# A fused two-layer graph kernel: the setup and first group rewritten, with a step table of its own

## The chip, the cores and the metric

The kernel runs on one core of one Trainium2 chip. Its time is the device time of one execution in microseconds (us). Before the change the median of three runs is 1575.77 us (1575.29 to 1577.64). The profile is of one further execution.

A core has five engines that run side by side, each through a queue of its own in order: TensorE (PE in the profile; PEld are its weight loads), VectorE (DVE), ScalarE (ACT), GpSimd (POOL) and SyncE (SP), which here only issues DMAs. An instruction at the head of a queue that waits for another engine holds everything behind it.

## What is computed

For each of 128 graphs of 128 nodes with 256 features:

```python
h = relu(layernorm(x))
x = x + adj @ (h @ W0) + b0                            # layer 0
h = relu(layernorm(x))
f = h @ fc_w + fc_b                                    # 8 heads of 256
logits = (f @ q_w + q_b) + (f @ k_w + k_b).T           # for each head
a = softmax(leaky_relu(logits + (1 - adj) * -1e9))
x = x + sigmoid(concat(a @ f) @ fp_w + fp_b + h)       # layer 1
```

All is float32. The kernel never makes f. The weights are folded first: for each head, q_w and k_w are multiplied into fc_w (the columns `wqk`), and fc_w times fp_w gives the 256x256 matrices held in `wts`.

## The kernel before

**Groups and periods.** Four graphs make a group (`GB`), so there are 32 groups, s0 to s31. A setup, written out by hand, loads and turns the weights and takes the first groups some way. Then a loop runs over the groups, one period each. A period has 44 slots, four units of 11; a unit is two graphs times half of the heads (`ORDER`, L595). In every slot PE does either one `aggregate` (L561: attention times h, output g_ps) or one `multiply` (L599: eight products with the folded weights of one of seven factors f0 to f6). The multiplies of a unit run in the slots of the next unit, so unit 0 of the first period has none. `take` (L572) turns g_ps into the factors: on ACT, or for (1, 0) on DVE with a difference on POOL. `combine` (L617) adds the sums up on DVE.

**The step table.** Beside the slots stands `PLAN` (L673): (slot, which group relative to the current one, step, arguments). In period g the attention of group g + 1 is made, the first layer of group g + 3 is computed, the second norm of g + 2 is applied, and so on. The loop (L906 to L935) first issues the slot's PE work, then the steps of that slot in the table's order. This order, by hand, is the order in every queue (the schedule is set to manual at L760). In the first period (g = 0) the steps in `LATE` (L756) are left out of PLAN, and `FIRST_PLAN` (L869) adds others for s0, s1, s2 and s3.

**Attention of one graph.** `masked` (L494) spreads the k values with a 32x32 block transpose on DVE (L489) and adds the mask, also on DVE (L497). `leaky` (L507) is eight ACT instructions, `head_max` (L515) one DVE reduction, `exps` (L523) eight ACT instructions, `normal` (L531) a small DVE reciprocal and a product on POOL (L535). `move` (L539) then carries the attention of two graphs, in 32x32 blocks, into another tile by 16 DMAs on SP (those of s0's first pair on SP and ACT), so that `turn` (L550), a DVE block transpose, makes a full transpose of it. h2 is turned the same way by `move_h2` and `turn_h2_blocks` (L421, L428), adj by `load_blocks` and `turn_blocks` (L73, L346). `turn_h2` (L435) and `turn_adj` (L352) do the same by PE transposes and ACT copies; before the change they are used for s0 and s1. `make_qk`, `turn_qk` and `load_k` (L448 to L481) make q and k, send k to memory on SP and read it back spread over the partitions (kq), which `masked` needs.

**The setup.** `setup_turn` (L171) transposes fc_w. `setup_wqk` (L183) makes wqk with 16 products for each half of the features, of two columns each. `setup_weights` (L207) folds fc_w and fp_w for one head and half and copies from PSUM on DVE or ACT. `setup_fb` (DVE, one block of fp_w at a time) and `setup_fb2` (POOL, the last blocks at once, L250) fold the bias; `NV` (L239) says where they part. `setup_sums` (L271) makes sums of the folded weights on POOL and DVE in turn.

PSUM tiles with the tag "m" share six banks (`ps_m`). Input tiles (xg, ag) have two buffers, so that the load of group n waits for the end of the first layer of group n - 2.

## Time and profile before

| | before |
|---|---|
| median of three runs | 1575.77 us |
| the profiled execution | 1576.38 us |
| its span, first to last instruction | 1574.2 us |
| mean granted TensorE clock | 0.979 |
| busy: PE, PEld | 1509.0, 1213.2 us |
| busy: DVE, ACT, POOL | 1228.9, 1173.8, 984.0 us |
| DMA moved | 142.07 MB, mean 90 GB/s |
| first masking of s0 (L489) starts | 42.56 us |
| first g_ps of the first period (L564) starts | 74.70 us |
| first take (L581) starts | 79.92 us |
| first masking of the second period (L489) starts | 146.83 us |

How to read it: "busy" is the time in which an engine executed, over the span. The page also cuts the span into 40 equal slices of some 39 us and prints the busy share of each in tenths, so a row of 9s is an engine that is busy throughout. "PEclk" is the TensorE clock that was granted, also in tenths. The stage table sums the same for stretches that one chooses, with the number of instructions in brackets. In the timeline a row is: start in us, duration or, for merged instructions, the stretch from first to last in us, engine, line of the kernel, operation, output<-inputs, shapes, count, and in square brackets how long the engine had been idle before and what ended that. SPq is SP's queue issuing DMAs. The chain of waits is the work that ended last, followed back from the end: each piece of it is what the next piece waited for.

### The profile page before, as it was taken

The numbers are of one execution on the slowest core, as the hardware profiler recorded it, in microseconds if no ns is written. First come the engines' busy times: TensorE is split into PE (matmuls) and PEld (weight loads), VectorE is DVE, ScalarE is ACT, GpSimd is POOL, SyncE is SP. The second block draws the span as 40 slices with busy tenths as digits, with TensorE's granted clock in tenths as the row PEclk, the third lists the DMA queues.
The fourth block names the chain that finished last, engine by engine and source line by source line (L and its number), as shares of the span: only waits on it lengthen the run. The fifth ranks groups of instructions, "written<-read, shape, count | busy, mean of one in ns | idle before, by whom it ended". The sixth has DMA issues, their size and how long they took to land.

```text
span 1574.2 us, 30745 instructions
## 1 busy us (share of the span) xinstructions
PE 1509.0 (96%) x9953; PEld 1213.2 (77%) x9953; DVE 1228.9 (78%) x2253; ACT 1173.8 (75%) x3889; POOL 984.0 (63%) x724
## 2 busy tenths in 40 slices
PE   7786999999999999999999999999999999999997
PEld 7565877887777878777777877777877777778776
DVE  5676778887777888777888877788887778887762
ACT  3683788777778877777987777897777789777751
POOL 3163766666676666676666667666666766666664
PEclk7888999999999999999999999999999999999999
DMA  5132434434444443444444344444434444433320
GB/s 181 34 88 63 104 84 97 94 90 88 101 93 97 95 93 78 102 104 90 97 93 95 80 102 105 87 98 92 94 82 101 107 83 98 92 78 80 73 68 27
DMA packets 259689, 142.07 MB, mean 90 GB/s; under 512 B 174901, under 2 KB 226505, under 8 KB 259273
## 3 DMA queue, kind: packets, MB, share of 16 engines
q1 hardware_dynamic: 259288, 139.79, 39.7%
q8 instruction: 78, 1.28, 0.4%
q14 instruction: 83, 0.67, 0.2%
q10 hardware_dynamic: 240, 0.33, 0.1%
HBM read 39.86 MB, written 17.30 MB: 36 GB/s over the span
## 4 chain that ended last, share of the span: by engine, by line
ACT 44%; PE 23%; DVE 16%; SPq 9%; issue 4%; DMA 2%; POOL 2%; ACTq 0%; POOLq 0%; DVEq 0%
ACT attn L526 18%; PE acc L609 11%; ACT attn L510 10%; SPq L546 6%; DVE attn L497 6%; ACT h L319 6%; PE x_ps L383 5%; PE g_ps L564 5%; DVE attn L489 5%; ACT f L589 2%; ACT L657 2%; ACT L526 2%; SPq L426 2%; ACT z L657 2%; DVE st L285 1%
## 5 line engine op out<-in xcount | busy, mean ns | idle before, releaser
L609 PEld LDWEIGHTS acc<-wts,f 128*128 128x128 f32 x7168 | 889.6, 192 | 281.2 <-issue 181.7
L609 PE MATMUL acc<-wts,f 128*128 128x128 f32 x7168 | 897.9, 276 | 23.8 <-DVE z L625 12.9
L564 PE MATMUL g_ps<-attnT,h 128*128 128x512 f32 x1024 | 530.1, 600 | 5.3 <-DVE attnT L553 3.3
L526 ACT ACTIVATE attn<-attn,nmax 128x128 f32<-128x128 f32 x1024 | 397.3, 396 | 0.4
L587 POOL TENSOR_TENSOR f<-f,f 128x512 f32<-128x512 f32 x128 | 163.2, 1275 | 286.7 <-DVE f L585 284.4
L510 ACT ACTIVATE attn<-attn,q 128x128 f32<-128x128 f32 x1024 | 312.9, 391 | 34.4 <-DVE attn L497 27.1
L535 POOL TENSOR_TENSOR attn<-attn,total 128x1024 f32<-128x1024 f32 x128 | 245.1, 1915 | 140.8 <-DVE total L534 140.8
L589 ACT COPY f<-g_ps 128x512 f32<-128x512 f32 x128 | 73.3, 572 | 241.1 <-PE g_ps L564 241.1
L518 DVE TENSOR_REDUCE nmax<-attn 128x8 f32<-128x1024 f32 x128 | 154.0, 1204 | 64.1 <-ACT attn L510 63.9
L526 ACT ACTIVATION_READ_ACCUMULATOR attn<-attn,nmax 128x1 f32 x1024 | 199.3, 195 | 0.0
L497 DVE TENSOR_TENSOR attn<-attn,mask 128x1024 f32<-128x1024 f32 x128 | 186.4, 1456 | 4.5
L590 POOL TENSOR_TENSOR f<-f,f 128x512 f32<-128x512 f32 x128 | 180.5, 1410 | 6.5 <-ACT f L589 3.9
L553 DVE STREAM_TRANSPOSE attnT<-attnB 128x1024 f32<-128x1024 f32 x128 | 153.3, 1218 | 39.7 <-DMA attnB<-attn 34.7
L489 DVE STREAM_TRANSPOSE attn<-kq 128x1024 f32<-128x1024 f32 x128 | 157.2, 1228 | 15.9 <-DMA kq<-k_mem 15.6
L564 PEld LDWEIGHTS g_ps<-attnT,h 128*128 128x128 f32 x1024 | 157.6, 194 | 13.8 <-issue 9.6
L383 PE MATMUL x_ps<-w_sb,ahT 128*128 128x256 f32 x512 | 124.2, 387 | 0.0
L585 DVE TENSOR_TENSOR f<-g_ps,f 128x512 f32<-128x512 f32 x128 | 87.1, 681 | 47.3 <-POOL attn L535 38.9
L661 POOL TENSOR_TENSOR z<-z,x 128x1024 f32<-128x1024 f32 (+1 forms) x33 | 76.2, 2310 | 56.3 <-ACT z L657 56.3
L653 POOL TENSOR_TENSOR z<-z,h 128x256 f32<-128x256 f32 x128 | 90.7, 731 | 23.3 <-DVE z L625 22.7
L581 ACT COPY f<-g_ps 128x512 f32<-128x512 f32 x128 | 74.0, 578 | 40.7 <-PE g_ps L564 39.6
L383 PEld LDWEIGHTS x_ps<-w_sb,ahT 128*128 128x128 f32 x512 | 93.5, 192 | 11.6 <-issue 0.7
L586 DVE TENSOR_TENSOR f<-f,g_ps 128x512 f32<-128x512 f32 x128 | 86.5, 676 | 0.0
(93 smaller groups left out, 1356.8 us busy)
## 6 DMA issues: line engine op xcount, KB each, us to landing
attnB<-attn SPq DMA_DIRECT2D x1019, 64.0 KB, 2.0
xg<-in_x_dram SPq DMA_DIRECT2D x32, 512.0 KB, 4.0
out_dram<-z SPq DMA_DIRECT2D x31, 512.0 KB, 3.1
h2B<-h SPq DMA_DIRECT2D x480, 32.0 KB, 1.9
ag<-in_adj_dram SPq DMA_DIRECT2D x32, 256.0 KB, 4.5
agB<-in_adj_dram SPq DMA_DIRECT2D x120, 64.0 KB, 4.5
fcw<-in_L_gnn_fc_w_dram SPq DMA_DIRECT2D x2, 1024.0 KB, 6.9
fpw<-in_L_gnn_fp_w_dram SPq DMA_DIRECT2D x1, 2048.0 KB, 14.1
```

The source lines that it names most:

```text
L383: nc.tensor.matmul(op[:, bb, :], lhsT=s["ahT"][:, 2 * b2 + bb, c, :], rhs=w0_sb[:, c, :], start=(c == 0), stop=(c == NC - 1),)
L489: nc.vector.transpose(s["a", b // 2][:, :, b % 2], s["kq"][:, :, b].unsqueeze(3).to_broadcast([P, NB, H, Q]),)
L497: nc.vector.tensor_tensor(a, a, s["mask"][:, b, :] .rearrange("p (j c) -> p j c", c=Q) .unsqueeze(2) .to_broadcast([P, NB, H, Q]), ALU.add,)
L510: nc.scalar.activation(a[:, :, h, :], a[:, :, h, :], AF.Prelu, bias=s["q"][:, b, h : h + 1], alpha=0.01,)
L518: nc.vector.tensor_reduce(nmax, a.rearrange("p j h c -> p h j c"), AX.XY, ALU.max, negate=True)
L526: nc.scalar.activation(a[:, :, h, :], a[:, :, h, :], AF.Exp, bias=s["nmax", b][:, h : h + 1], accum_out=s["total", b][:, h : h + 1],)
L535: nc.gpsimd.tensor_tensor(a, a, total.unsqueeze(1).unsqueeze(3).to_broadcast([P, NB, H, Q]), ALU.mult)
L553: nc.vector.transpose(aT.rearrange("p h (i r) -> p i h r", r=Q), s["ab", b // 2][:, :, b % 2])
L564: nc.tensor.matmul(u["g", b, c], lhsT=s["h2"][:, 2 * pair + b].rearrange("p j c q -> p (j c q)")[:, ts(c, P)], rhs=s["aT", 2 * pair + b][: ...
L587: nc.gpsimd.tensor_tensor(new(5), f[4], f[0], ALU.subtract)
L590: nc.gpsimd.tensor_tensor(new(2), f[1], f[5], ALU.subtract)
L609: nc.tensor.matmul(acc[:, slot, :], lhsT=u["f"][m][:, h, :], rhs=wt[m][:, half * HU + h, :], start=(half == 0 and h == 0 and m in FIRST), ...
```

## The change

The change rewrites the setup from `setup_wqk` on, gives the first period a complete table of its own, and leaves PLAN, which rules all later periods, as it is.

- `setup_wqk` makes rows instead of columns: for each half n of the heads and each g of four, 2 products with a 32-column stationary operand (`qkc`: q_w, k_w, and zeros) and 256 columns of fcwT, written to the partitions of column group g. `setup_wqk_turn` transposes the rows on PE into wqk_p.
- `NV` is NK - 8 instead of NK - 4: POOL's `setup_fb2` folds 8 blocks of the bias and DVE's `setup_fb` 8 instead of 12.
- s0's attention tile is laid out by heads (`view`), so that `turn_by_products` can transpose each head on PE, with one copy on ACT and one on DVE. s0 has no more `move` and `turn`. Other groups keep the layout by blocks.
- In the first period s2's adj and h2 are turned on PE (`turn_adj`, `turn_h2`), s3 takes the agB blocks, and s0's second half and all of s1's attention stand at new slots. In the setup the order of the folded weights, the bias, both `setup_sums` and s1's first layer is new.

The setup and the table before can be read in the listing above (L797 to L904).

```diff
--- before.py
+++ after.py
@@ -136,6 +136,9 @@
     cols = sp.tile([P, ROWS], FP, name="cols")
     mq = sp.tile([P, 1], FP, name="mq")
     mk = sp.tile([P, 1], FP, name="mk")
+    qkc = sp.tile([P, NC, Q], FP, name="qkc")
+    nc.gpsimd.memset(qkc, 0.0)
+    wqk_rows = sp.tile([P, 2, D], FP, name="wqk_rows")
     ones = sp.tile([P, P], FP, name="ones")
     nc.gpsimd.memset(ones, 1.0)
@@ -180,25 +183,38 @@
                 tp.rearrange("p k (j q) -> p k j q", q=Q),
             )
-    def setup_wqk(c):
-        qk_cols = cols[:, NK:ROWS].rearrange("p (two c) -> p c two", two=2)
-        wp = ps_m.tile([P, H, 2], FP, name="wp", tag="m")
-        for h in range(H):
-            for kk in range(NC):
-                nc.tensor.matmul(
-                    wp[:, h, :],
-                    lhsT=fcwT[:, NC * h + kk, ts(c, P)],
-                    rhs=qk_cols[:, kk, :],
-                    start=(kk == 0),
-                    stop=(kk == NC - 1),
-                )
+    def setup_wqk():
         nc.vector.tensor_copy(
-            wqk_p[:, c, 0 : 2 * H].rearrange("p (two h) -> p two h", two=2),
-            wp.rearrange("p h two -> p two h"),
-        )
-    def setup_wqk_order():
+            qkc[:, :, 0:2], cols[:, NK:ROWS].rearrange("p (two c) -> p c two", two=2)
+        )
+        wp = ps_m.tile([P, 2, D], FP, name="wp", tag="m")
+        for n in range(2):
+            for g in range(4):
+                for kk in range(NC):
+                    nc.tensor.matmul(
+                        wp[ts(g, Q), n, :],
+                        lhsT=qkc[:, kk, :],
+                        rhs=fcwT[:, NC * (4 * n + g) + kk, :],
+                        start=(kk == 0),
+                        stop=(kk == NC - 1),
+                    )
+        nc.vector.tensor_copy(wqk_rows, wp)
+    def setup_wqk_turn():
+        tp = ps_m.tile([P, 2, NC, P], FP, name="wt_ps", tag="m")
+        for n in range(2):
+            for c in range(NC):
+                nc.tensor.transpose(tp[:, n, c, :], wqk_rows[:, n, ts(c, P)], ident)
+        for c in range(NC):
+            nc.vector.tensor_copy(
+                wqk_p[:, c, 0 : 2 * H].rearrange("p (two n g) -> p n two g", two=2, n=2),
+                tp[:, :, c].rearrange("p n (g r) -> p n r g", r=Q)[:, :, 0:2],
+            )
+    def setup_wqk_order(_):
         for j in range(NB):
             for c in range(NC):
                 n = 2 * (j % 2) + c
@@ -236,7 +252,7 @@
-    NV = NK - 4
+    NV = NK - 8
     fb = sp.tile([P, D], FP, name="fb")
     fb2 = sp.tile([P, NK - NV, D], FP, name="fb2")
@@ -482,18 +498,27 @@
+    def view(s, b):
+        a = s["a", b // 2]
+        if s["g"]:
+            a = a.rearrange("p (j b h c) -> p b j h c", j=NB, b=2, c=Q)
+        else:
+            a = a.rearrange("p (b h j c) -> p b j h c", j=NB, b=2, c=Q)
+        s["v", b] = a[:, b % 2]
     def spread(s, b):
         if b % 2 == 0:
-            s["a", b // 2] = at.tile([P, NB, 2, H, Q], FP, name="attn", tag="attn", bufs=3)
+            s["a", b // 2] = at.tile([P, 2 * H * P], FP, name="attn", tag="attn", bufs=3)
+        view(s, b)
         nc.vector.transpose(
-            s["a", b // 2][:, :, b % 2],
+            s["v", b],
             s["kq"][:, :, b].unsqueeze(3).to_broadcast([P, NB, H, Q]),
         )
     def masked(s, b):
         spread(s, b)
-        a = s["a", b // 2][:, :, b % 2]
+        a = s["v", b]
         nc.vector.tensor_tensor(
             a,
             a,
...
@@ -544,7 +569,8 @@
         for n in blocks:
             i, j = divmod(n, NB)
             queues[n % len(queues)].dma_start(
-                s["ab", pair][ts(j, Q), i], s["a", pair][ts(i, Q), j]
+                s["ab", pair][ts(j, Q), i],
+                s["a", pair][ts(i, Q)].rearrange("p (j n) -> p j n", j=NB)[:, j],
             )
     def turn(s, b):
@@ -553,6 +579,17 @@
         nc.vector.transpose(
             aT.rearrange("p h (i r) -> p i h r", r=Q), s["ab", b // 2][:, :, b % 2]
         )
+    def turn_by_products(s, b):
+        aT = s["aT", b] = pool["attnT"].tile([P, H, P], FP, name="attnT", tag="attnT")
+        for h4 in range(2):
+            tp = ps_m.tile([P, 4, P], FP, name="aT_ps", tag="m")
+            for h in range(4):
+                n = H * (b % 2) + 4 * h4 + h
+                nc.tensor.transpose(tp[:, h, :], s["a", b // 2][:, ts(n, P)], ident)
+            copy = nc.vector.tensor_copy if h4 else nc.scalar.copy
+            copy(aT[:, ts(h4, 4)], tp)
@@ -753,7 +790,99 @@
         (43, 0, residual_a, 1),
     ]
-    LATE = (shift_both, n2_apply, move_h2, turn_h2_blocks, make_qk, turn_qk, load_k, turn)
+    FIRST_PLAN = [
+        (0, "u", take, 0, 0, 0),
+        (0, 3, load_blocks),
+        (0, 0, exps, 2, 0, H),
+        (3, "u", take, 0, 1, 1),
+        (3, 0, head_max, 3),
+        (7, "u", take, 0, 1, 0),
+        (9, "u", take, 0, 0, 1),
+        (9, 0, normal, 2),
+        (9, 0, exps, 3, 0, H),
+        (11, "u", take, 1, 0, 0),
+        (12, 2, turn_adj),
+        (12, 2, make_mask),
+        (14, "u", take, 1, 1, 1),
+        (14, 1, masked, 0),
+        (15, 0, normal, 3),
+        (15, 2, n1_apply, 0),
+        (15, 2, n1_apply, 1),
+        (15, 2, add_b0),
+        (16, 0, turn_by_products, 2),
+        (17, "u", take, 1, 1, 0),
+        (17, 1, leaky, 0),
+        (18, 0, turn_by_products, 3),
+        (18, 3, n1_stats, 0),
+        (18, 3, n1_stats, 1),
+        (20, "u", take, 1, 0, 1),
+        (20, 1, masked, 1),
+        (20, 2, first_a, 0),
+        (20, 2, first_a, 1),
+        (21, 0, residual_a, 0),
+        (22, "u", take, 2, 0, 0),
+        (22, 1, leaky, 1),
+        (22, 1, head_max, 0),
+        (22, 1, exps, 0, 0, H),
+        (23, 2, first_b, 0),
+        (23, 2, first_b, 1),
+        (24, 4, begin),
+        (24, 2, n2_stats, 0),
+        (24, 2, n2_stats, 1),
+        (24, 2, rdev_both),
+        (25, "u", take, 2, 1, 1),
+        (25, 1, head_max, 1),
+        (25, 1, normal, 0),
+        (25, 2, shift_both),
+        (26, 2, n2_apply, 0),
+        (26, 2, n2_apply, 1),
+        (26, 1, exps, 1, 0, H),
+        (26, 1, masked, 2),
+        (27, "u", combine, 1, 4),
+        (28, "u", take, 2, 1, 0),
+        (28, 2, turn_h2, 0),
+        (28, 2, turn_h2, 1),
+        (28, 1, normal, 1),
+        (28, 1, move, 0),
+        (28, 1, leaky, 2),
+        (31, "u", take, 2, 0, 1),
+        (31, 3, n1_apply, 0),
+        (31, 3, n1_apply, 1),
+        (31, 3, add_b0),
+        (31, 1, masked, 3),
+        (32, 2, make_qk, wqk_p),
+        (32, 1, head_max, 2),
+        (32, "u", combine, 1, 2),
+        (32, 0, residual_b, 0),
+        (33, "u", take, 3, 0, 0),
+        (33, 1, exps, 2, 0, H),
+        (33, 1, leaky, 3),
+        (34, 2, turn_qk),
+        (34, 2, load_k),
+        (34, 3, turn_blocks),
+        (36, "u", take, 3, 1, 1),
+        (36, 0, setup_wqk_order),
+        (36, 4, n1_stats, 0),
+        (36, 4, n1_stats, 1),
+        (36, 1, head_max, 3),
+        (36, 1, normal, 2),
+        (37, 3, first_a, 0),
+        (37, 3, first_a, 1),
+        (37, 1, exps, 3, 0, H),
+        (38, 1, turn, 0),
+        (39, "u", take, 3, 1, 0),
+        (39, 3, first_b, 0),
+        (39, 3, n2_stats, 0),
+        (39, 1, turn, 1),
+        (39, 1, normal, 3),
+        (40, 1, move, 1),
+        (41, 3, first_b, 1),
+        (41, 3, n2_stats, 1),
+        (41, 3, rdev_both),
+        (42, "u", take, 3, 0, 1),
+        (42, 3, make_mask),
+        (43, 0, residual_a, 1),
+    ]
     groups = [{"g": g} for g in range(NG)]
     pool = {}
@@ -794,114 +923,83 @@
     pool["attnT"] = ctx.enter_context(tc.tile_pool(name="attnT", bufs=4, side="right"))
     n2_apply(s0, 0)
     n2_apply(s0, 1)
+    setup_wqk()
     for half in range(2):
         n1_stats(s1, half)
     scale((s1, "n1"), root=True)
+    turn_h2(s0, 0)
+    turn_h2(s0, 1)
+    setup_wqk_turn()
     setup_bias()
     begin(s2)
-    setup_fb2()
-    for k in range(NV):
-        setup_fb(k)
-    setup_wqk(0)
-    turn_h2(s0, 0)
-    turn_h2(s0, 1)
-    setup_wqk(1)
+    for half in range(2):
+        n1_apply(s1, half)
+    make_mask(s1)
+    add_b0(s1)
     make_qk(s0, wqk_p)
+    turn_adj(s1)
     turn_qk(s0)
     load_k(s0)
-    for half in range(2):
-        n1_apply(s1, half)
-    turn_adj(s1)
-    make_mask(s1)
-    add_b0(s1)
+    setup_fb2()
+    for h in range(2):
+        setup_weights(h, 0, False)
+        setup_weights(h, 1, False)
+    first_a(s1, 0)
+    first_a(s1, 1)
     for half in range(2):
         n1_stats(s2, half)
-    first_a(s1, 0)
-    first_a(s1, 1)
+    for k in range(3):
+        setup_fb(k)
     masked(s0, 0)
     leaky(s0, 0)
     masked(s0, 1)
+    first_b(s1, 0)
     leaky(s0, 1)
-    first_b(s1, 0)
-    first_b(s1, 1)
     head_max(s0, 0)
     exps(s0, 0, 0, H)
+    first_b(s1, 1)
     head_max(s0, 1)
     exps(s0, 1, 0, H)
-    setup_weights(0, 0, True)
+    begin(s3)
+    setup_weights(2, 0, True)
+    n2_stats(s1, 0)
+    setup_weights(2, 1, True)
+    n2_stats(s1, 1)
+    rdev((s1, "n2"), (s2, "n1"))
+    setup_weights(3, 0, True)
+    setup_weights(3, 1, True)
+    setup_weights(4, 0, True)
     normal(s0, 0)
-    n2_stats(s1, 0)
-    setup_weights(0, 1, True)
-    n2_stats(s1, 1)
-    setup_weights(1, 0, True)
-    scale((s1, "n2"), (s2, "n1"))
+    shift((s1, "n2"), (s2, "n1"))
+    setup_weights(4, 1, True)
+    setup_weights(5, 0, True)
+    setup_weights(5, 1, True)
     normal(s0, 1)
-    setup_weights(1, 1, True)
+    masked(s0, 2)
     for half in range(2):
         n2_apply(s1, half)
-    for h in range(2, 4):
-        setup_weights(h, 0, True)
-        setup_weights(h, 1, True)
+    turn_by_products(s0, 0)
     turn_h2(s1, 0)
     turn_h2(s1, 1)
-    move(s0, 0, queues=(nc.sync, nc.sync, nc.scalar))
-    setup_weights(4, 0, True)
-    setup_weights(4, 1, True)
+    for k in range(3, NV):
+        setup_fb(k)
+    turn_by_products(s0, 1)
     make_qk(s1, wqk_p)
-    setup_wqk_order()
-    masked(s0, 2)
-    for h in range(5, H):
-        setup_weights(h, 0, False)
-        setup_weights(h, 1, False)
     leaky(s0, 2)
     masked(s0, 3)
-    leaky(s0, 3)
+    setup_weights(6, 0, True)
+    setup_weights(6, 1, False)
+    head_max(s0, 2)
     turn_qk(s1)
     load_k(s1)
-    turn(s0, 0)
-    turn(s0, 1)
-    head_max(s0, 2)
+    setup_weights(7, 0, True)
+    setup_weights(7, 1, False)
+    leaky(s0, 3)
+    setup_sums(0)
     setup_fpb()
-    setup_sums(0)
-    exps(s0, 2, 0, H)
+    setup_sums(1)
     setup.close()
     pool["un"] = ctx.enter_context(tc.tile_pool(name="unit", bufs=2))
...
     units = [None]
     for g in range(NG):
         cur = groups[g]
@@ -915,12 +1013,8 @@
                 aggregate(units[n], o[1], o[2])
             elif n or last:
                 multiply(units[n - 1] if n else last, o)
-            if g == 0:
-                for at_, f, *args in FIRST_PLAN:
-                    if at_ == slot:
-                        f(*args)
-            for at_, who, f, *args in PLAN:
-                if at_ != slot or (g == 0 and f in LATE):
+            for at_, who, f, *args in PLAN if g else FIRST_PLAN:
+                if at_ != slot:
                     continue
                 if who == "u":
                     u = last if args[0] < 0 else units[args[0]]
```

Lines with "..." stand for what is cut: `masked`, `leaky`, `head_max`, `exps` and `normal` take the tile from `s["v", b]`, and the table of before goes.

More of the change, by code (lines that the diff above doesn't have):

```diff
@@ L507, in leaky @@
     def leaky(s, b, h0=0, nh=H):
-        a = s["a", b // 2][:, :, b % 2]
+        a = s["v", b]
         for h in range(h0, h0 + nh):
@@ L515, in head_max @@
     def head_max(s, b):
-        a = s["a", b // 2][:, :, b % 2]
+        a = s["v", b]
         nmax = s["nmax", b] = small.tile([P, H], FP, name="nmax", tag="nmax", bufs=4)
@@ L523, in exps @@
     def exps(s, b, h0, nh):
-        a = s["a", b // 2][:, :, b % 2]
+        a = s["v", b]
         for h in range(h0, h0 + nh):
@@ L531, in normal @@
     def normal(s, b):
-        a = s["a", b // 2][:, :, b % 2]
+        a = s["v", b]
         total = s["total", b]
@@ L859, in gnn_then_gat_kernel @@
+    head_max(s0, 2)
     turn_qk(s1)
     load_k(s1)
-    turn(s0, 0)
-    turn(s0, 1)
-    head_max(s0, 2)
+    setup_weights(7, 0, True)
+    setup_weights(7, 1, False)
+    leaky(s0, 3)
+    setup_sums(0)
     setup_fpb()
-    setup_sums(0)
-    exps(s0, 2, 0, H)
+    setup_sums(1)
     setup.close()
     pool["un"] = ctx.enter_context(tc.tile_pool(name="unit", bufs=2))
-    FIRST_PLAN = [
-        (0, load_blocks, s2),
-        (1, begin, s3),
-        (1, turn_blocks, s2),
-        (1, normal, s0, 2),
-        (1, head_max, s0, 3),
-        (1, n1_apply, s2, 0),
-        (1, n1_apply, s2, 1),
-        (2, exps, s0, 3, 0, H),
-        (2, add_b0, s2),
-        (6, normal, s0, 3),
-        (6, move, s0, 1),
-        (4, first_a, s2, 0),
-        (4, first_a, s2, 1),
-        (7, setup_sums, 1),
-        (7, make_mask, s2),
-        (7, n1_stats, s3, 0),
-        (9, first_b, s2, 0),
-        (9, n1_stats, s3, 1),
-        (9, n2_stats, s2, 0),
-        (11, first_b, s2, 1),
-        (11, n2_stats, s2, 1),
-        (11, rdev_both, s2),
-        (13, turn, s0, 2),
-        (13, turn, s0, 3),
-        (13, shift_both, s2),
-        (16, n2_apply, s2, 0),
-        (16, n2_apply, s2, 1),
-        (16, move_h2, s2),
-        (34, turn_h2_blocks, s2),
-        (38, make_qk, s2),
-        (40, turn_qk, s2),
-        (40, load_k, s2),
-        (41, turn, s1, 0),
-        (41, turn, s1, 1),
-    ]
```

## The prediction

> **What bounds the kernel now.** I read the page's slices first, then busy time by stage, then the timeline where a stage has holes. The span is 1574.2 us, the profiled execution 1576.38 (2.2 lie around the span), the median of the three runs 1575.77, 0.6 below it. I sum against the profiled execution and take 0.6 off at the end. A measurement of this kernel can tell about 0.2% (3.2 us) from no change.
>
> ```profile
> PE   7786999999999999999999999999999999999997
> PEclk7888999999999999999999999999999999999999
> ```
>
> Only the first four slices (39 us each) have holes. By stage (us, busy PE, PEld, DVE, ACT, POOL, granted clock, DMA share, GB/s):
>
> ```profile
> 20.00:45.00 25.00, 23.18 (x115) 21.71 (x116) 15.56 (x43) 8.27 (x17) 6.91 (x5) 0.53 0.19 41
> 45.00:75.00 30.00, 22.69 (x106) 17.70 (x105) 20.42 (x48) 20.55 (x71) 6.72 (x4) 0.88 0.16 36
> 75.00:98.00 23.00, 16.57 (x67) 11.33 (x66) 19.50 (x26) 22.57 (x88) 12.15 (x9) 0.70 0.31 72
> 120.00:145.00 25.00, 24.09 (x164) 19.30 (x163) 14.02 (x33) 4.83 (x10) 12.73 (x10) 1.00 0.39 88
> 145.00:160.00 15.00, 3.96 (x18) 3.55 (x17) 12.96 (x19) 10.63 (x38) 2.55 (x2) 0.59 0.12 19
> 206.00:252.00 46.00, 45.40 (x306) 36.53 (x305) 37.60 (x69) 36.38 (x121) 30.39 (x23) 1.00 0.43 95
> ```
>
> In a later period PE works 45.4 of 46.0 us. The chain of waits shows one masking per period:
>
> ```profile
> 242.76 2.25 DVE attn L497
> 288.86 2.25 DVE attn L497
> 334.97 2.26 DVE attn L497
> ```
>
> 46.1 us apart, and the change touches no instruction of those periods. So what it can win lies ahead of about 174 us, where the second period (g = 1) reaches slot 27 (L634 at 174.0; 115.3 in the first). From there the time to the end is taken as fixed.
>
> Why the second period starts late, from the timeline:
>
> ```profile
> 119.73 22.15 SPq L546 DMA_DIRECT2D attnB<-attn  x32
> 141.99 0.53 SPq L473 DMA_DIRECT2D k_mem<-k  x1
> 143.63 1.73 SPq L478 DMA_DIRECT2D kq<-k_mem  x4
> 146.83 1.25 DVE L489 STREAM_TRANSPOSE attn<-kq 128x1024 f32<-128x1024 f32 x1 [11.07 <-DMA kq<-k_mem]
> 156.48 3.76 PE L609 MATMUL acc<-wts,f 128*128 128x128 f32 x16 [11.04 <-DVE z L625]
> ```
>
> 32 block moves at 0.69 us each fill SP's queue; k of group 2 was ready at 129.9 and is stored at 142. DVE waits 11 us for it at the head of its queue, and PE 11 us behind DVE. That is one hole. The others: ACT starts attention only at 45.2, and the first take is at 79.9.
>
> **The change, part by part.**
>
> *q_w and k_w.* Removed: 64 matmul records of L189, 13.1 us (20.7 to 35.4), all ahead of the first make_qk. Added: 32 records of 256 columns in column groups. The nearest row is make_qk, which has the same form:
>
> ```profile
> 35.33 1.44 PE L453 MATMUL qk_ps<-h2T,wqk_p 128*32 128x128 f32 x16
> 65.78 0.66 PE L453 MATMUL qk_ps<-h2T,wqk_p 128*32 128x128 f32 x16
> ```
>
> Twice the records and columns: 5.8 us at the clock of 0.5 granted at 35, 2.6 at full clock. One group after the other would be 32 x 0.236 = 7.6 (L383, full clock) to 15.1. Here a rule has to be weighed: the Trainium skill ("TensorE: Matmul & The Clock Gate", Part 1: The HAM clock gate) gives the full clock after some 3.4 us of sustained matmuls, so that 2.6 would hold. The stage 20 to 45 shows PE busy 23.2 of 25.0 us at a mean clock of 0.53, so busy alone doesn't lift it. I take 5.8; the two differ by 3.2 us here. Then a PSUM copy (0.69), four transposes (0.5 to 1), two small copies. DVE is held at the head of its queue by the PSUM copy, with n1_stats of group 1 (2.1) and its norm (0.75) behind. I get: products done 27.7, copy 28.5, norm 31.3, make_qk 32, k ready 33.9, against 37.9. The kq round trip (37.95 to 42.56) puts the first masking at 38.5, 4 us earlier.
>
> *setup_fb2 on 8 blocks instead of 4.* This takes the 4 us back. POOL's product grows from 1.90 to 3.8, the sums from 2.07 to 1.9 + 1.27 + 0.72: a train from 36.3 (after add_b0) to 44. Before, it ran at 21 to 25, beside nothing that minded. Now three setup_fb and masked(0) stand beside it. What one such meeting costs:
>
> ```profile
> 85.94 2.36 POOL L337 TENSOR_TENSOR xg<-xg,b_bc 128x1024 f32<-128x1024 f32 x1
> 87.39 1.99 DVE L497 TENSOR_TENSOR attn<-attn,mask 128x1024 f32<-128x1024 f32 x1
> ```
>
> 1.99 instead of 1.23, and it ends 1.08 after POOL's end (88.30): it did its work after POOL was done. The longest L497 of the trace is 2.27, so the rows alone charge at most 1.0 a meeting. The Trainium skill ("SBUF — State Buffer", Who interferes with whom) speaks against the change: a DVE instruction with two SBUF inputs and a GpSimd one exclude each other for a whole instruction. Then the wait is up to 3.8, and the two engines alternate: setup_fb 1 ends 40.5, setup_fb 2 42.7, masked(0) 45.5 instead of 40.9. By the row's 1.0 it would end near 42. I take 45.5: L497's end follows POOL's end, as the rule has it. Before, it was 45.1, so this stage wins nothing.
>
> *To the first take.* ACT from 45.6: two leaky (2.45 each), table 1.28, two exps (3.1 each) to 58.0; n2_apply 2.1, a copy of turn_by_products 0.55, two of h2T 1.05, another copy 0.5, leaky(2) 2.45: 64.7. DVE beside it: masked(2) is held by normal(1) on POOL (58.3 to 60.2) and ends 61.3; copy 0.7, five setup_fb 2.6 + 0.5, copy 0.7, qk 0.3: 66.1; masked(3) 68.5. leaky(3) ends 70.95, and the first take is at 71 instead of 79.9. The 32 moves of group 0 are gone, with five issues on ACT's queue (3.3) and four DVE transposes (1.2 each); for them come 32 transposes on PE (4, in its holes), four DVE copies (0.7) and four ACT copies (0.57).
>
> *To slot 27.* DVE: weights, head_max(2), k and q, setup_sums(0), fpb to 72.4; setup_sums(1) waits for POOL's chain to 74.5; head_max(3) ends 77.0, take 78.2. POOL: 587, 590 to 80.1; masked(s1,0) takes its turn to 81.1; normal(2) 83.0, mask 83.7, normal(3) 85.6, add_b0 87.9. The PE transposes of pair 1 (slots 16, 18) wait for these two normals, with the multiplies behind: 84.0 and 86.9, some 3 us of PE. Then DVE: n1_stats(s3) 89.7, masked(s1,1) behind residual_a 93.1, head_max 94.3, first_b and n2_stats of s2 100.5, POOL's power 102.4, shift, masked(s1,2) behind normal 105.4: combine at 105.4 against 115.3. Moved along are begin(s4) on SP (two DMAs, slot 24) and turn_adj, turn_h2 of group 2 (12 transposes, 1.5 on PE; 1.7 on ACT) for 20 DMAs (4 agB, 16 h2B).
>
> *To the second period.* Group 1's attention, earlier in the table of before, is what is late next. ACT: exps(1) 107.9, h2T 108.9, leaky(2) 111.4, take, n1_apply(s3) 113.9, take, exps(2) 117.5, leaky(3) 120.0, take, two ahT 121.5, exps(3) 124.6. SP: move(s1,0) 110.1 to 121.1, landed 123; load_k only behind it, kq at 126. DVE: turn 0 at 124.2, take, first_b, n2_stats, turn 1 128.3, to rdev 130.4. So masked(s2,0) starts at 130.4 instead of 146.8: 16.4 won. Held by POOL's power, it ends 133.1 against 149.3.
>
> *Inside the second period.* move(s1,1) leaves SP at 130.4 to 141.4, and move_h2 only behind it, to 151.9, landed 153.8. turn_h2_blocks stands in slot 18, due about 149.8: DVE waits up to 4, with normal and head_max behind it. Between 0 (PE has its factors) and 4 I take 2.4, since the chain of waits has h2B among its landings. Won: 16.2 - 2.4 = 13.8. Slot 27 comes at 160.2; 1576.4 - 13.8 = 1562.6, less 0.6: 1562.0. The edits to view and normal are addresses only for g > 0; qkc's memset (0.15, as L103) lies in POOL's idle start: nothing.
>
> **Rivals.** *POOL costs little* (0.22): the meetings cost what the rows show. For: POOL is busy in only 13.6 of the 55 us from 20 to 75. Against: L497's end at 87.39. Then 4 come back at masked(0) and about 4 of the later holds: 1554. *SP's queue is the new wait* (0.16): all 4 of turn_h2_blocks and 3 more for group 1's turns come through. For: SP issues some 60 DMAs a period, about 40 of 46 us. Against: 52 DMAs have gone before. 1569. *The column groups do nothing* (0.05): they run one after the other, 15.1 instead of 5.8. k is ready at 43, masked(0) ends 50: 1567. L453 speaks against it. *Slower* (0.05): the periods start in another phase, in which one more masking per period meets a POOL instruction, as one of four already does (2.25): 1.03 x 30 periods = 31, 1593. It decides from 13.8 / 30 = 0.46 us a period. Against: from the third period on they are 46.1 whatever the start was.
>
> **The numbers.** The likeliest, 1562, has 0.52 and itself reaches from 1557 to 1567. The range 1551 to 1571 takes in most of the first three rivals and leaves out the slow one. Faster 0.92; same 0.03 (the far end of the SP case); slower 0.05.
>
> **What would show it.** Right: L189's place taken by about 6 us of PE; L497 of group 0 ending near 45 behind POOL's sums; first take near 71; L634 of g = 0 near 105; L489 of g = 1 near 130, no longer waiting for kq; 46.1 between later periods. Wrong: a first masking that ends at 41, a wait of over 4 us on h2B, or another period.

## The result and the profile after

The changed kernel takes 1560.24 us (median of four runs, 1559.79 to 1562.91) against 1575.53 beside it: a ratio of 0.9906 (95% interval 0.9889 to 0.9923). The forecast was 1562.0. The profiled execution took 1560.45 us with a span of 1558.6, at a mean granted clock of 0.991 (0.979 before).

The page's slices after: busy tenths of PE, and the granted clock in tenths.

```profile
PE   6788999999999999999999999999999999999997
PEclk9889999999999999999999999999999999999999
```

PE's four slices with holes are still there. The first has even fewer busy tenths than before (6 against 7): the new products keep PE busy for a shorter time than the old ones. The stages of the table, at the same times of the span as before (us, busy PE, PEld, DVE, ACT, POOL, clock, DMA share, GB/s):

```profile
20.00:45.00 25.00, 19.32 (x133) 15.58 (x133) 18.80 (x39) 10.86 (x26) 10.43 (x5) 0.93 0.18 41
...
120.00:145.00 25.00, 23.85 (x154) 19.29 (x153) 24.34 (x51) 17.82 (x64) 14.03 (x9) 1.00 0.28 62
145.00:160.00 15.00, 11.82 (x92) 9.43 (x91) 10.01 (x15) 15.00 (x64) 8.24 (x7) 1.00 0.53 104
206.00:252.00 46.00, 45.42 (x306) 36.52 (x305) 37.69 (x69) 36.37 (x122) 30.51 (x22) 1.00 0.43 94
```

The hole at 145 to 160 has closed from 11.0 us of idle PE to 3.2, and the clock of the first stage rose from 0.53 to 0.93. The later period is as it was. The timeline in the order of the prediction's steps (start, duration, both us):

```profile
22.18 3.46 PE L196 MATMUL wp<-fcwT,qkc 128*32 128x256 f32 x32 [3.28 <-DVE qkc L189]
34.21 3.65 POOL L268 TENSOR_TENSOR fb<-fpw,cols 128x2048 f32<-128x2048 f32 x1
34.44 6.20 DVE L264 SCALAR_TENSOR_TENSOR fb<-fpw,cols,fb 128x256 f32<-128x256 f32 x2
37.94 4.63 POOL L273 TENSOR_TENSOR fb<-fb 128x1024 f32<-128x1024 f32 x3
41.90 1.75 DVE L522 TENSOR_TENSOR attn<-attn,mask 128x1024 f32<-128x1024 f32 x1
131.37 1.23 DVE L514 STREAM_TRANSPOSE attn<-kq 128x1024 f32<-128x1024 f32 x1
131.38 10.45 SPq L571 DMA_DIRECT2D attnB<-attn  x16
141.94 11.71 SPq L442 DMA_DIRECT2D h2B<-h  x16
```

L522 is the mask's addition (L497 before), L514 the spread (L489), L571 the moves (L546). The two `setup_fb` on DVE take 6.20 us together, and the masking (41.90 + 1.75) ends at 43.65, 1.1 after POOL's train (37.94 + 4.63, so 42.57). The second period's spread starts at 131.37 and waits for no kq. What the train and the moves leave over are the longest waits between 132 and 168 us that concern h2B (total, times, longest):

```profile
PE qk_ps L469 <- DVE h2T L446: 3.2, 1, 3.2
DVE h2T L446 <- DMA h2B<-h: 2.9, 1, 2.9
```

| mark, us | before | predicted | after |
|---|---|---|---|
| k of s0 ready | 37.95 | 33.9 | 31.57 |
| masked(s0, 0) ends | 45.13 | 45.5 | 43.65 |
| first take starts | 79.92 | 71 | 69.90 |
| slot 27, g = 0 | 115.31 | 105.4 | 106.50 |
| masked(s2, 0) starts, g = 1 | 146.83 | 130.4 | 131.37 |
| slot 27, g = 1 | 174.03 | 160.2 | 159.81 |

The lead over before is 6.4 us at k, 1.5 at the end of the first masking, 10.0 at the first take, 8.8 in the first period's slot 27, 15.5 at the second period's masking and 14.2 in its slot 27. It is 14.1 in the third period and then grows in small steps to 15.5 in the last.

### The profile page after: what moved, and what is told of

The parts are those of the page before. It is cut to its first block, busy times and chain, and to the rows that moved or that the text cites. A ratio compares the mean times of both kernels' runs of the same rounds, so it can differ in the third digit from the quotient of the medians.

```text
span 1558.6 us, 30703 instructions
## 1 busy us (share of the span) xinstructions
PE 1498.8 (96%) x9969; PEld 1203.1 (77%) x9969; DVE 1237.1 (79%) x2249; ACT 1177.6 (76%) x3896; POOL 991.5 (64%) x726
## 4 chain that ended last, share of the span: by engine, by line
ACT 40%; PE 20%; DVE 17%; SPq 13%; issue 4%; POOL 3%; DMA 2%; ACTq 0%; POOLq 0%; DVEq 0%
ACT attn L551 16%; PE acc L646 10%; SPq L571 10%; ACT attn L535 10%; DVE attn L522 6%; ACT h L335 5%; PE x_ps L399 5%; PE g_ps L601 4%; DVE attn L514 4%; SPq L442 2%; ACT f L626 2%; ACT L694 2%; ACT L551 2%; DVE st L301 1%; POOL attn L560 1%
## 5 line engine op out<-in xcount | busy, mean ns | idle before, releaser
L646 PEld LDWEIGHTS acc<-wts,f 128*128 128x128 f32 x7168 | 889.1, 192 | 271.4 <-issue 179.6
L646 PE MATMUL acc<-wts,f 128*128 128x128 f32 x7168 | 897.7, 276 | 15.1 <-ACT f L626 11.0
L522 DVE TENSOR_TENSOR attn<-attn,mask 128x1024 f32<-128x1024 f32 x128 | 189.1, 1477 | 4.5
L579 DVE STREAM_TRANSPOSE attnT<-attnB 128x1024 f32<-128x1024 f32 x124 | 148.7, 1218 | 38.7 <-DMA attnB<-attn 37.0
L514 DVE STREAM_TRANSPOSE attn<-kq 128x1024 f32<-128x1024 f32 x128 | 156.9, 1226 | 2.5 <-DMA kq<-k_mem 2.4
L353 POOL TENSOR_TENSOR xg<-xg,b_bc 128x1024 f32<-128x1024 f32 x32 | 75.5, 2359 | 17.8 <-ACT h L335 17.8
```

Source lines behind the costliest of these rows:

```text
L514: nc.vector.transpose(s["v", b], s["kq"][:, :, b].unsqueeze(3).to_broadcast([P, NB, H, Q]),)
L522: nc.vector.tensor_tensor(a, a, s["mask"][:, b, :] .rearrange("p (j c) -> p j c", c=Q) .unsqueeze(2) .to_broadcast([P, NB, H, Q]), ALU.add,)
L646: nc.tensor.matmul(acc[:, slot, :], lhsT=u["f"][m][:, h, :], rhs=wt[m][:, half * HU + h, :], start=(half == 0 and h == 0 and m in FIRST), ...
```

## The experiments

**Theory.** The lead has three sources: the earlier k, group 0's and group 2's turns on PE instead of in SP's queue, and what follows from these in the second period. POOL's train gives part of the start back. **First rival:** the start's gain is swallowed on the way, and SP's queue makes all of the lead. **Second rival:** turning group 0 on PE is worth little, since its moves lie beside other work. The medians before, in every set of runs, lie between 1574.75 and 1575.53.

### The old q_w and k_w products in the new setup (old_wqk)

```diff
-    setup_wqk()
+    setup_wqk_old(0)
...
-    setup_wqk_turn()
+    setup_wqk_old(1)
```

> The changed kernel with the old setup_wqk (64 two-column products in place of 32 in column groups and four transposes). Theory (POOL's bias train takes back what the column groups give): k is ready about 6.5 us later (38 instead of 31.5), but the first masking, which the train already held back until 43.6, ends only some 2 to 3 us later (45.5 to 46.5), and slot 27 of the second period (159.8 in the changed kernel) comes 2 to 3 us later. Rival (the column groups carry the start): everything comes 6.5 us later, slot 27 at 166.

`setup_wqk_old` is the function of before. Measured: 1562.75 (1561.4 to 1568.42), interval of the ratio [0.9900, 0.9941], so 2.5 us above the change in medians, with intervals that overlap. k is ready at 39.85 instead of 31.57, but the masking ends only 3.5 later (47.19), and the first take is 4.3 later. Of the 8.3 us won at k, 4.7 don't reach the masking, which stands behind POOL's train anyway. But slot 27 of the second period comes at 167.91, 8.1 later, which is the rival's figure and not the theory's. The profiled execution was the longest of its four (1568.42). Beside the 4.3 us at the first take, it loses 1.3 on the way to the first slot 27, where it has 9.2 us at the half clock (6.1 in the change), and 2.6 in the second period, where it has 6.8 (none in the change). So the theory holds at the masking and in the median; how much the column groups bring at the end, this run doesn't settle.

### The old share of POOL in the bias (fb2_four)

```diff
-    NV = NK - 8
+    NV = NK - 4
```

> The changed kernel with NV = NK - 4, so that POOL folds 4 blocks of the bias at once and DVE 12. Theory (a DVE instruction with two SBUF inputs waits for a whole POOL instruction): the train is 3.9 us instead of 8, the second and third setup_fb end near 37.5, the first masking ends near 40 instead of 43.6; four more setup_fb on DVE later take back 2.1, so slot 27 of the second period moves by -1 to -2 us. Rival (a meeting costs at most what the rows of before show, 1 us): the first masking ends at 42.5 or later, and with the four added instructions slot 27 comes 1 us later.

Measured: 1557.98 (1556.45 to 1562.09), [0.9872, 0.9911]. The masking ends 3.6 us earlier (40.03), slot 27 of the second period comes 4.0 earlier (155.84), and the median is 2.3 lower. The rival is out: it had the masking at 42.5 or later. The larger share delays the masking within the change, but not all of the 4.0 is its price. The first take is 1.5 earlier, and another 1.6 come where this execution had no half clock and the change's had 6.1 us of it. The intervals of the two medians overlap, so that the larger share costs time at the end is likely, not shown.

### POOL's train earlier (fb2_early, then fb2_idle)

```diff
     n2_apply(s0, 1)
+    setup_fb2()
     setup_wqk()
...
     load_k(s0)
-    setup_fb2()
```

> The changed kernel with setup_fb2 issued ahead of setup_wqk, where POOL is idle (from the landing of fp_w at about 21), so that the train ends near 29. Theory: three setup_fb run unheld from 33.7 to 35.2, the first masking ends at 38.5 instead of 43.6, and nearly all of these 5 us arrive at slot 27 of the second period (155 to 156); total 1555.5. Rival (the early stage has slack, and ACT or the moves of group 1 set the pace): the masking ends early, but less than 2 us arrive at slot 27; total 1559.

Measured: 1561.98 (1560.71 to 1562.38), [0.9893, 0.9922]: no gain. The timeline of fb2_early shows why:

```profile
21.16 3.60 POOL L268 TENSOR_TENSOR fb<-fpw,cols 128x2048 f32<-128x2048 f32 x1 [8.22 <-DMA fpw<-in_L_gnn_fp_w_dram]
21.71 3.08 DVE L189 COPY qkc<-cols 128x4 f32<-128x4 f32 x1
24.93 3.60 PE L196 MATMUL wp<-fcwT,qkc 128*32 128x256 f32 x32 [6.19 <-DVE qkc L189]
```

A copy of 4 elements a partition, 0.16 us in the change, lasts 3.08: it ends just after POOL's product (24.76). It has one input, where the rule in the prediction speaks of two. PE's products wait for it, and k is 2.9 later than in the change. The train was moved from one victim to another. Even so the masking ends 2.1 earlier (41.60). What was left of this at slot 27 of the first period, 0.8, is lost in the second: there a gap of PE ends at the half clock (154.6 to 161.4), and slot 27 comes at 161.64, 1.8 later than in the change. So the next kernel takes that copy out of `setup_wqk` and issues it where DVE is idle, with `setup_fb2` early as in fb2_early:

```diff
         nc.vector.tensor_copy(cols, cp)
+        nc.vector.tensor_copy(
+            qkc[:, :, 0:2], cols[:, NK:ROWS].rearrange("p (two c) -> p c two", two=2)
+        )
```

> The changed kernel with setup_fb2 ahead of setup_wqk, as in the run fb2_early, and the copy into qkc moved up to where DVE is idle (right after the copy into cols), so that POOL's first long product no longer holds it for 3 us. Theory: k stays at 31.5, the three setup_fb run unheld, the first masking ends at 38.6 instead of 43.6 and slot 27 of the first period comes 4 to 5 us earlier (102); total 1556. Rival (something else takes the time back before slot 27): slot 27 of the first period less than 2 us earlier.

Measured: 1558.69 (four runs, 1552.2, 1558.29, 1559.08 and 1559.85), [0.9866, 0.9913]. Its timeline:

```profile
21.39 2.48 PE L196 MATMUL wp<-fcwT,qkc 128*32 128x256 f32 x32 [1.97 <-ACT fcwT L184]
32.75 1.01 DVE L264 SCALAR_TENSOR_TENSOR fb<-fpw,cols,fb 128x256 f32<-128x256 f32 x2
36.02 1.23 DVE L522 TENSOR_TENSOR attn<-attn,mask 128x1024 f32<-128x1024 f32 x1
```

With POOL idle, two `setup_fb` cost 1.01 instead of 6.20 and the mask 1.23 instead of 1.75; the masking ends at 37.24, 6.4 earlier. Slot 27 of the first period comes 8.0 earlier (98.51). The median moved by 1.5 only. The profiled execution was the fastest of the four (1552.2) and ran 12.0 us of its span at the half clock, where the change's had 28.0. Its mean granted clock was 0.996; that of the other three was 0.991 and 0.992. So the start is won in the profiled execution, and how much reaches the end differs by 7.7 us between executions of this one kernel.

### Group 0 by block moves again (moves_s0)

The layout by blocks comes back too (`view`, not shown).

```diff
-        (16, 0, turn_by_products, 2),
+        (16, 0, move, 1),
...
-        (18, 0, turn_by_products, 3),
...
+        (21, 0, turn, 2),
+        (21, 0, turn, 3),
...
-    turn_by_products(s0, 0)
+    move(s0, 0)
...
-    turn_by_products(s0, 1)
...
     leaky(s0, 3)
+    turn(s0, 0)
+    turn(s0, 1)
```

> The changed kernel with group 0's attention laid out by blocks again and turned by 32 block moves on SP and four DVE transposes, instead of the PE transposes; the moves stand where the PE transposes stood, the DVE transposes just ahead of the slots that need them. Theory: 16 moves take SP 11 us and 2 to land, so the first take comes at 75 to 77 instead of 69.9 and pair 1 some 8 us later; slot 27 of the second period 7 to 10 us later (167 to 170). Rival (the gain is SP's queue for group 1 alone, which these moves don't touch as they end before it): no more than 3 us later.

Measured: 1573.2 (1572.02 to 1574.78), [0.9978, 0.9994], 13 us above the change. That is more than the theory's 7 to 10 us, and the second rival is out for this table. The first take is 4.5 later (74.42). In its timeline:

```profile
88.71 10.01 SPq L568 DMA_DIRECT2D attnB<-attn  x16
100.24 2.37 DVE L576 STREAM_TRANSPOSE attnT<-attnB 128x1024 f32<-128x1024 f32 x2 [8.17 <-DMA attnB<-attn]
101.63 2.05 PE L598 MATMUL g_ps<-attnT,h 128*128 128x512 f32 x2 [11.69 <-DVE attnT L576]
```

The moves start when `normal` is done (88.68) and take 10 us to issue. DVE stands idle 8.2 us for their landing at the head of its queue, PE 11.7 behind it. Slot 27 comes at 118.77, later even than before. The turns' slots are of my choosing, so part of the 13 belongs to where they stand in this table and not to the moves as such.

### Group 2's h2 by block moves again (s2_moves)

```diff
+        (26, 2, move_h2),
...
-        (28, 2, turn_h2, 0),
-        (28, 2, turn_h2, 1),
...
+        (31, 2, turn_h2_blocks),
```

> The changed kernel with h2 of group 2 turned by 16 moves on SP and a DVE transpose in the first period (as in the kernel before), instead of PE transposes. Theory (SP's queue is the last to come at the end of the first period): the moves go out at 106 to 116, group 1's moves behind them at 116 to 126 instead of 111.5 to 121.6, and the second period starts 4 to 5 us later, slot 27 at 164 to 165, total 1564.5. Rival (SP has room there): less than 1.5 us later.

Measured: 1566.44 (1565.35 to 1567.3), [0.9931, 0.9960], so 6.2 above the change. SP's queue in its trace:

```profile
107.58 10.41 SPq L442 DMA_DIRECT2D h2B<-h  x16
118.09 10.75 SPq L571 DMA_DIRECT2D attnB<-attn  x16
128.94 0.52 SPq L489 DMA_DIRECT2D k_mem<-k  x1
```

Sixteen issues ahead of group 1's moves push k's store from 121.7 to 128.9, and the second period's masking starts at 139.5 instead of 131.4. But the masking waits for no kq in either kernel, and the queue is not the only thing that is late:

```profile
119.61 1.25 DVE L446 STREAM_TRANSPOSE h2T<-h2B 128x1024 f32<-128x1024 f32 x1 [5.67 <-DMA h2B<-h]
121.01 1.11 PE L469 MATMUL qk_ps<-h2T,wqk_p 128*32 128x128 f32 x16 [14.39 <-DVE h2T L446]
125.92 0.19 DVE L485 COPY k<-q_ps 128x32 f32<-128x32 f32 x1 [0.94 <-PE q_ps L483]
```

DVE stands idle 5.7 us until h2's blocks have landed, and PE 14.4 us for the turned h2. make_qk comes at 121.0 (112.2 in the change), and k is ready at 126.1 (118.0), so it then waits only 2.8 us for SP, less than the 3.7 in the change. The theory's result came, larger than expected, but mostly by another way: h2's own way through SP and back holds DVE and PE. The 6.2 us are the price of that way as a whole, not of k's place in the queue.

### The second period's h2 by PE as well (h2_by_pe)

```diff
+    SECOND_PLAN = []
+    for at_, who, f, *args in PLAN:
+        if f is turn_h2_blocks:
+            SECOND_PLAN += [(at_, who, turn_h2, 0), (at_, who, turn_h2, 1)]
+        elif f is make_qk:
+            SECOND_PLAN.append((at_, who, f, wqk_p))
+        elif f is not move_h2:
+            SECOND_PLAN.append((at_, who, f, *args))
...
-            for at_, who, f, *args in PLAN if g else FIRST_PLAN:
+            for at_, who, f, *args in (FIRST_PLAN, SECOND_PLAN, PLAN)[min(g, 2)]:
```

> The changed kernel, and in the second period too h2 (of group 3) is turned by PE transposes and ACT copies at slot 18, in place of 16 moves on SP and a DVE transpose. Theory (SP's queue, with 16 attention moves and then 16 h2 moves back to back, makes the second period late: PE waits 3 us for h2 at 153, and where this gap ends with the clock at half, 2.7 more): the gap goes, slot 27 of the second period comes at 156.5 to 157.5 instead of 159.8, total 1556 to 1557.5. Rival (the wait only takes the place of another one, and PE and ACT have 1 us more to do): slot 27 no more than 1 us earlier, total 1559.5.

Measured: 1559.04 (1557.91 to 1560.58), [0.9881, 0.9914]. PE's wait for the turned h2 is gone, and from the masking's end to slot 27 it takes 24.3 us instead of 25.95. The median fell by 1.2, about what the runs scatter, and is the rival's (1559.5) rather than the theory's; in its profile the first period was 1.8 later, with the same table up to there.

### Train early and h2 by PE together (both)

fb2_idle and h2_by_pe in one kernel, with no other edit.

> The two edits of h2_by_pe and fb2_idle together. Theory (they act in different stages, so they add): slot 27 of the second period at 152 to 153, total 1552 to 1553. Rival (one queue sets both): no better than the better one of the two, 1556.

Measured: 1552.62 (1550.97 to 1557.14), [0.9843, 0.9885], 7.6 below the change and within the theory's total. Slot 27 of the second period comes at 154.35, 5.5 earlier than in the change (the theory had 152 to 153). In the stage from 145 to 160 us PE has no hole left:

```profile
145.00:160.00 15.00, 15.00 (x111) 11.81 (x111) 9.01 (x20) 15.00 (x62) 11.82 (x8) 1.00 0.24 54
```

Apart, the two edits gave 1.5 and 1.2; together 7.6. I cannot show from these runs why the sum is more than the parts: the executions of fb2_idle scatter by more than this, and its interval overlaps that of both. One reading fits: where PE's gap behind h2 ended at the half clock (fb2_early, old_wqk), the second period took 2.6 us longer, and without the gap this can't happen. The slower executions of fb2_idle have no trace that could tell.

### One part alone, on the kernel before (wqk_alone, start_only, k_first)

The new q_w and k_w products in the place of the old ones:

```diff
-    setup_wqk(0)
+    setup_wqk()
     turn_h2(s0, 0)
     turn_h2(s0, 1)
-    setup_wqk(1)
+    setup_wqk_turn()
```

> The kernel before with one part of the change alone: setup_wqk by column groups and its transposes. Here POOL's bias train runs early (21 to 25), but DVE's 12 setup_fb (25 to 31.5) stand ahead of the bias of q and k. Theory (this part moves the start, the larger gain is in how group 0 is turned): k is ready at 33.5 to 34.5 instead of 37.95, everything up to the second period moves with it, total 1572, 3.5 less than before. Rival (column groups bring most of the gain of 15): total 1563 or less.

Measured: 1577.65 (1575.38 to 1580.16), [1.0008, 1.0026]: slightly slower, and the expectation is missed by 7 us at k, which is ready at 41.13. Its timeline:

```profile
28.01 5.69 DVE L264 SCALAR_TENSOR_TENSOR fb<-fpw,cols,fb 128x256 f32<-128x256 f32 x11
33.62 0.16 DVE L189 COPY qkc<-cols 128x4 f32<-128x4 f32 x1
33.93 3.64 PE L196 MATMUL wp<-fcwT,qkc 128*32 128x256 f32 x32 [13.77 <-DVE qkc L189]
```

The products need a copy on DVE that the old ones didn't, and there it stands behind `setup_fb`. PE is idle 13.8 us for it. The median lies 2.9 us above the 1574.75 beside it, which is small but clear of the noise. I had costed the products and forgotten that their operand has a place in a queue. With the copy and the products early, and nine of the `setup_fb` later:

```diff
         nc.vector.tensor_copy(cols, cp)
+        nc.vector.tensor_copy(
+            qkc[:, :, 0:2], cols[:, NK:ROWS].rearrange("p (two c) -> p c two", two=2)
+        )
...
     n2_apply(s0, 1)
+    setup_wqk()
...
-    for k in range(NV):
-        setup_fb(k)
-    setup_wqk(0)
     turn_h2(s0, 0)
     turn_h2(s0, 1)
-    setup_wqk(1)
+    setup_wqk_turn()
...
+    for k in range(3):
+        setup_fb(k)
     masked(s0, 0)
...
+    for k in range(3, NV):
+        setup_fb(k)
     turn_h2(s1, 0)
```

> The kernel before with the start alone changed: setup_wqk by column groups right after n2_apply, its DVE copy into qkc early, and setup_fb moved from ahead of q and k (3 in front of the first masking, 9 behind n2_apply of group 1). Group 0 is still turned by moves, and the first period has its old table. This mends the run wqk_alone, in which 12 setup_fb stood ahead of qkc in DVE's queue. Theory (an earlier start is passed on whole, since the first period is a chain): k ready at 30 to 31.5, first masking ends at 38 instead of 45.1, everything up to slot 27 of the second period 6 to 7 us earlier (167 to 168), total 1568. Rival (SP's queue of moves sets the second period, so an earlier start is lost there): less than 3 us, 1572 or more.

Measured: 1569.29 (1569.24 to 1571.62), [0.9957, 0.9983], 6.1 below before. k is ready at 30.67, the masking ends at 38.0 (7.1 earlier), slot 27 of the second period comes 6.4 earlier. With nothing else changed, this start is passed on nearly whole, and for it the first rival is out. It isn't the start of the change, though: here POOL's train stays early, as in the kernel before. In the change the train takes most of k's lead, and the masking is only 1.5 earlier than before. Last, SP's order alone, which is no part of the change but takes away the same wait:

```diff
         (40, load_k, s2),
+        (40, move, s1, 1, range(6, 16)),
...
-                if at_ != slot or (g == 0 and f in LATE):
+                if at_ != slot or (g == 0 and f in LATE) or (g == 0 and slot == 34 and f is move):
```

> The kernel before, with the last 10 block moves of group 1 issued in slot 40 behind the store and loads of group 2's k instead of ahead of them. Theory (SP's queue held k for 12 us, and DVE, PE and ACT behind it): the first masking of the second period starts at 141 to 142 instead of 146.8, slot 27 comes some 4 us earlier, total 1571. Rival (another queue is late at the same place, or the later moves make slot 12's turns late): less than 1.5 us earlier.

Measured: 1566.98 (1566.84 to 1569.08), [0.9937, 0.9970], 8.4 below before and twice what I expected. Its trace, SP's queue and the spread:

```profile
133.64 0.53 SPq L473 DMA_DIRECT2D k_mem<-k  x1
135.28 2.90 SPq L478 DMA_DIRECT2D kq<-k_mem  x4
138.23 6.23 SPq L546 DMA_DIRECT2D attnB<-attn  x10
139.71 1.25 DVE L489 STREAM_TRANSPOSE attn<-kq 128x1024 f32<-128x1024 f32 x1 [4.88 <-DMA kq<-k_mem]
```

Ten moves put behind five DMAs start the second period's attention 7.1 us earlier, and the moved ten are late for nobody.

### Three more reorderings (best)

On top of both, four steps are moved:

```diff
+        (7, 0, normal, 2),
         (7, "u", take, 0, 1, 0),
         (9, "u", take, 0, 0, 1),
-        (9, 0, normal, 2),
...
-        (25, 1, normal, 0),
         (25, 2, shift_both),
+        (25, 1, normal, 0),
...
-    normal(s0, 0)
     shift((s1, "n2"), (s2, "n1"))
+    normal(s0, 0)
...
-    setup_sums(1)
...
+            if g == 0 and slot == 10:
+                setup_sums(1)
```

> The kernel of the run both, with three pairs of steps in another order: shift ahead of normal (twice), since shift on DVE was held for the whole 1.9 us of normal on POOL; setup_sums(1) behind the first takes (slot 10); normal(2) of group 0 ahead of the take of slot 7, so that the PE transposes of slot 16 don't wait for it behind two other POOL products. Theory: 1.7 + 1.7 of the holds and 1 to 3 us of PE's wait at slot 16 go, slot 27 of the second period 3 to 5 us earlier than in both, total 1548 to 1549.5. Rival (SP's moves of group 1, or ACT, take the place): total within 1 us of both.

Measured: 1555.72 (1551.78, 1555.35, 1557.02, 1556.09), [0.9859, 0.9888]. In its profile slot 27 of the second period comes 2.75 us before that of both, but the median is higher, the expected 1548 to 1549.5 is missed, and the intervals overlap. This run decides nothing; both stays the best kernel that I can name.

## Why the prediction was right

**q_w and k_w.** The form was right and the term too large: 3.46 us instead of 5.8, at the half clock that was assumed. With the steps behind it, which went as said, k is 2.3 early. The scaling from make_qk holds at the full clock (2.6 predicted, 2.48 in fb2_idle) and fails at the half one. The row at 35.33 holds a wait of 0.15 us for wqk_p, which is too little to explain it, and the rest stays open. The clock in two windows, before and after:

```profile
21.40:25.30 3.90, 3.90 (x20) 3.90 (x21) 3.33 (x14) 1.97 (x5) 3.72 (x3) 0.51 0.59 172
25.30:45.30 20.00, 18.85 (x91) 17.37 (x92) 11.34 (x28) 5.03 (x10) 3.02 (x2) 0.50 0.03 5
...
21.90:25.30 3.40, 3.12 (x32) 1.68 (x32) 0.13 (x2) 1.38 (x3) 0.00 (x0) 0.50 0.45 136
25.30:45.30 20.00, 16.19 (x109) 13.90 (x101) 17.46 (x33) 7.93 (x20) 10.43 (x5) 1.00 0.03 5
```

After, one window of 3.4 us is at 0.50, then 20 us at 1.00. Before, the clock stayed at 0.50 to 0.51 from 21.4 to 45.3 with PE busy 22.75 of the 23.9 us. old_wqk, with the old products in the new setup, has the half clock from 24.3 to 44.8 with PE busy 19.7 of 20.5 us, so it is the products that make the difference. The rule of the Trainium skill ("TensorE: Matmul & The Clock Gate", Part 1: The HAM clock gate) puts the first 3.4 us or so of sustained work at the half clock and what follows at the full one. For the wide products the trace agrees; the two-column ones kept PE busy without lifting the clock. The prediction drew too much from the rule: products that take about as long as this warm-up themselves could not all have run at full clock by it. What the full clock brought behind 25.3 no run separates from the shorter products. Nor do they tell which property of the products counts as work.

**POOL's train.** Right, in place, size and mechanism: whole instructions exclude each other and the engines alternate, as L264 (6.20 for two) and L522 (ending 1.1 after the train) show. The masking came 1.85 early because the train itself started 2.1 early: it stands behind group 1's norm and add_b0, which moved up with the shorter products. Here the rule ("SBUF — State Buffer", Who interferes with whom) had been chosen over the row's 1.0 a meeting, and the rule was right. The rival *POOL costs little* is out: fb2_four, fb2_idle and start_only, which shorten the train or put it earlier, all end the masking between 37.2 and 40.0.

**To the first take and slot 27.** The take is 1.1 early (69.90), of a 1.85 lead. From the masking to the take the lead over before grows from 1.5 to 10.0; moves_s0 gives 4.5 of this back. I put the rest down to the new order of the setup, which no run takes out. Slot 27 is 1.1 late, so this stage took 36.6 us instead of 34.4. My sum had no half clock in it; of this stage 83.3 to 86.7 and 103.8 to 106.5 ran at half. Other runs with the same steps in this stage (s2_moves adds moves on SP at its end) show what that costs:

| first take to slot 27, g = 0 | at half clock, us | the stage, us |
|---|---|---|
| fb2_four, fb2_idle | 0.0, 0.6 | 35.0, 35.0 |
| s2_moves, the change | 3.4, 6.1 | 36.6, 36.6 |
| old_wqk, fb2_early, h2_by_pe, both | 9.1 to 9.3 | 37.8 to 37.9 |

From fb2_four to the change PE's busy time in this stage grows from 26.95 to 28.71 us, and that of DVE and POOL stays the same. So 1.6 of the 2.2 us go with the half clock.

**To the second period.** Predicted 130.4, measured 131.37: 1.0 late, as slot 27 was. The step as such, SP's queue with k behind 16 moves instead of 48, is right: the spread waits for no kq any more, and DVE's own queue leads up to it. k_first shows the price of k's old place, 7.1 us at the masking; the 8.1 of s2_moves are mostly h2's own way. This is the second period's hole from which the prediction started.

**h2B.** Predicted between 0 and 4, taken 2.4; DVE waited 2.9 and PE 3.2. The rival *SP's queue is the new wait* charged 7. h2_by_pe takes the wait away and wins 1.65 in that stretch.

**The rest.** 13.8 predicted as won at slot 27, 14.2 measured. The 1.3 us that came later were not predicted; they come as three steps (0.35, 0.2 and 0.7 at 387, 1171 and 1491 us of the span before) in which a period of before lasts longer than the same one after, and which execution has them may be chance. So of the 1.8 between 1562.0 and 1560.24 only 0.4 belong to the steps. *Slower*: the later periods are still 46.1 us.

**What the prediction couldn't see.** Errors of opposite sign met: k 2.3 early, the way to slot 27 2.2 late. That the sum came out so close is in part luck, since this stage alone took 35.0 to 37.9 us in the runs above. And the parts don't add as its ledger suggests. start_only gives 6.1 and k_first 8.4, together 14.5, which looks like the whole change's 15.3. But neither is a part of the change: start_only wins 7.1 at the masking, where the change wins 1.5, and k_first keeps all the moves. To take group 0's PE turns out of the change costs 13. I take it that these stand behind each other in one chain, and that each is worth what the others let through; this isn't shown. start_only and k_first in one kernel were not tried.

## What to carry to other kernels

Price a new instruction with its operand's way to it: the products were cheap, and a copy of 4 elements behind a full queue made them dearer than the old ones (wqk_alone), and a POOL instruction beside it took back 2.9 us of what they won (fb2_early). Look at what a queue of transfers carries ahead of the one that opens the next stage: ten moves put behind five DMAs won 8.4 us with no work saved. When a change wins, take its parts back one at a time all the same: one here (POOL's larger share) delayed the first masking by 3.6 us and was probably a loss. And look at the granted clock before comparing two profiles: in one and the same stage, differences of up to 2.9 us went with it here.

## What the runs showed of the hardware

- A DVE copy of 128x4 next to a POOL product of 3.60 us lasted 3.08 us instead of 0.16 (fb2_early), so here the hold didn't depend on how little the DVE instruction had to move.
- 32 float32 products of 256 columns in four column groups took 3.46 us at the half clock (the change) and 2.48 at the full one (fb2_idle, granted clock 1.00 from 20 to 45 us), a ratio of 1.4 and not 2.
- The clock fell to half at 21.4 us in the kernel before although PE had been at its two-column products since 20.67. Before the wide products PE stood idle 1.97 us in fb2_idle and in both; in fb2_idle the clock stayed full (2.48 us), in both it fell to half at 21.8, in the midst of them (3.87 us).
- The time at half clock within the span differed between profiled executions from 12.0 us (fb2_idle) over 28.0 (the change) to 47.2 (old_wqk); before had 64.6. A PE gap near 154 us sometimes ended at half clock: 16 products of L646 behind it took 1.80 us in the change's chain of waits and 3.40 in fb2_early's. Executions of one kernel lay 3.1 us (the change) to 7.7 us (fb2_idle) apart, so smaller differences between single executions say little.
